# Maxima of four heads in one transfer with early fills, and one division per pair of heads: a decoder layer on one core

## Chip, cores and metric

One core of a Trainium2 chip. The metric is the device time of one execution in microseconds, median over the runs; lower is better. Before the change: 663.38 us, median of three runs (662.83, 663.38 and 667.53).

## What is computed

A decoder layer on x of shape (4, 1024, 256): windowed causal self-attention, cross-attention to 77 context rows, and a fake-quantised feed-forward part, each with a layer norm in front and added to x. Cut to what matters here:

```
# self-attention: 16 heads of 16, windows of 128, keys of this window and the one before
scores = einsum('bhcqd,bhckd->bhcqk', qc, kcat) / 4
scores = where(mask, scores, -inf)
attn   = softmax(scores, axis=-1)
out    = einsum('bhcqk,bhckd->bhcqd', attn, vcat)
x      = x + out @ w_out
# cross-attention: the same with 77 context rows as keys, a mask and biases
# feed-forward: quantised gate, up and down products
```

The softmax is computed as exp(score - max of its row), and the sum of a row comes out of the product with the values, as one more column of ones; the result is divided by it at the end.

## The kernel before

**Jobs, units, slots.** Attention is eight jobs in the order S0, S1, S2, X0, S3, X1, X2, X3: self-attention (S) and cross-attention (X) of the four batch entries. A job has two groups g of eight heads; in a group, head 2j + o lies in partitions 32j + 16o to 32j + 16o + 15, so o = 0 or 1 tells the even from the odd heads, and four heads (j = 0 to 3) run side by side on TensorE, each on 32 rows. A unit is (job, g, o, u): u runs over four quarters of the sequence in an S job and two halves in an X job. That makes 96 units, and slot n works on unit n. Within a slot the order of instructions on all engines is written out: products of weights and values that are due (weighted_values, normalise, by_features), then tasks by due time (project, values, out_project, transposes of x), then statistics and other DVE work beside, then put_maxima, then the maxima of the unit five slots ahead (LEAD = 5), then the weights of this slot's unit. A planner picks tasks by due time and cost; most of them come well ahead of their use.

**Maxima as a row of q.** The subtraction of the maximum is done by the product itself. For the heads of o, one row of each 32 (row 16 for o = 0, row 0 for o = 1) is free: q holds the negated maxima there and k holds ones. So a unit's scores are computed twice: in maxima (sc_n, query rows in partitions, line 735 for S and 750 for X) to find the largest score per query on DVE (lines 765 and 776), and in weights (sc_t, transposed, lines 827 and 856) with the maxima already in the product, followed by the exponential on ScalarE. While the maxima are sought, the free row must add nothing: q or k is zero in it.

**project** (line 346) computes q or k of one group and one half of the sequence. ScalarE copies the product twice: once whole and once with all rows but those of o set to zero (lines 377 and 378; for the q of an X job lines 364 and 367). For X jobs the zeros and ones of the free rows are filled here by two transfers per half (line 371).

**put_maxima** (line 784) runs once per (job, g, o), one slot (S) or three (X) before the first unit that needs it: TensorE turns the maxima into 32 rows of 128 (ps_mx), ScalarE copies them to mxT, and SyncE's queue sends, for S jobs, one fill of ones into k (line 793, four rows of 4 KB), then one transfer for each of the four heads j into its row of q (line 801, 4 KB each). All these transfers go through SyncE, one after another.

**weighted_values, normalise, by_features** (lines 862, 897, 912). The product with the values (ps_av) comes out with features in partitions. DVE transposes it in 32x32 blocks (o_sb, line 895), takes the reciprocal of the sums (rec, line 903), multiplies (aN, line 905), and after o = 1 transposes aN back (aT, line 917), which out_project (line 919) multiplies by the output weights. All of it stands at the head of a slot, ahead of the DVE reductions of that slot's maxima. o_sb has one buffer, aN two. In the last slots (tail) the multiplication goes to GpSimd.

PSUM has eight banks in rotation for all products, so that a product waits for the engine that reads the bank's old content.

Of the kernel before, what the change touches and what calls it, by code (L numbers as in the profile page):

```python
# [9 lines left out]
F32 = mybir.dt.float32  # L10
# [3 lines left out]
AF = mybir.ActivationFunctionType  # L14
ALU = mybir.AluOpType
# [3 lines left out]
P = 128  # L19
# [6 lines left out]
def decoder_layer(  # L26
# [44 lines left out]
    HS = S // NH  # L71
# [130 lines left out]
    with ExitStack() as att:  # L202
# [14 lines left out]
        rows, onerow, nextrow = [], [], []  # L217
# [68 lines left out]
        class Job:  # L286


            def __init__(self, kind, b):
                self.kind, self.b = kind, b  # L290
                self.leads = (kind, b) == ("S", 0)
                self.st = {}
                self.xn, self.xnT, self.vs, self.q, self.k = {}, {}, {}, {}, {}
                self.aN, self.aT, self.mx, self.pts, self.av = {}, {}, {}, {}, {}

            def branch(self):
                twin = copy.copy(self)
# [33 lines left out]
        def normed_T(job, hf):  # L331
# [11 lines left out]
                    nc.scalar.copy(xnT[:, c, :], ps)  # L343
            job.xnT[hf] = xnT

        def project(job, g, which, hf):
# [15 lines left out]
            half = [out[g, o][:, hf * HS : (hf + 1) * HS] for o in range(NS)]  # L362
            if job.kind == "X":
                nc.scalar.activation(
                    half[1], ps, AF.Identity, bias=job.bq[:, g : g + 1], scale=QSCALE
                )
                nc.scalar.activation(
                    half[0], half[1], AF.Identity, bias=nextrow[0], scale=rows[0]
                )
                for row in range(2):  # L370
                    queue_of[0].dma_start(
                        out=half[1][row : P : SL, :].rearrange("j (t q) -> j t q", q=P),
                        in_=none_one[row].unsqueeze(1).to_broadcast([NJ, HT, P]),
                    )
                return
            first = 1 if which == "q" else 0
            nc.scalar.activation(half[first], ps, AF.Copy, scale=QSCALE if which == "q" else 1.0)  # L377
            nc.scalar.activation(half[1 - first], half[first], AF.Copy, scale=rows[1 - first])


        leading = Job("S", 0)
# [34 lines left out]

        begun = dict(turn)
        begin.close()
        queue_of = [nc.sync]

        def attention(alike):
            turn.update(begun)
            queue_of[0] = nc.sync if alike else nc.scalar
# [360 lines left out]
            def put_maxima(job, g, o):  # L784

                ps = bank("ps_mx")
                nc.tensor.transpose(
                    ps[: NJ * NT, :P], job.mx[g, o].rearrange("p j t -> p (j t)"), ident
                )
                mxT = work.tile([NJ * NT, P], F32, name="mxT", tag="mxT", bufs=2)  # L790
                nc.scalar.copy(mxT, ps[: NJ * NT, :P])  # L791
                if job.kind == "S":
                    queue_of[0].dma_start(
                        out=job.k[g, o][(1 - o) * HD : P : SL, :].rearrange(
                            "j (t q) -> j t q", q=P
                        ),
                        in_=none_one[1].unsqueeze(1).to_broadcast([NJ, NT, P]),
                    )
                for j in range(NJ):
                    row = j * SL + (1 - o) * HD  # L800
                    queue_of[0].dma_start(
                        out=job.q[g, o][row : row + 1, :],
                        in_=mxT[j * NT : (j + 1) * NT, :],
                    )

            def weight_bias(job, g, o, u):

# [8 lines left out]
            def weights(job, g, o, u):  # L816
# [34 lines left out]
                else:  # L851
# [5 lines left out]
                    for j in range(NJ):  # L857
                        pt = work.tile([SK, HS], F32, name="ptx", tag="pt", bufs=16)
                        nc.scalar.activation(pt, banks[j][:SK], AF.Exp)  # L859
                        job.pts[g, o, j, u] = pt  # L860

            def weighted_values(job, g, o, hf):
                ps = bank("ps_av")
                heads = [2 * NJ * g + 2 * j + o for j in range(NJ)]
                if job.kind == "S":
                    t0 = hf * HT
                    for kb in range(max(t0 - 1, 0), t0 + HT):

                        a0, a1 = max(kb, t0), min(kb + 2, t0 + HT)
                        for j in range(NJ):  # L870
                            nc.tensor.matmul(  # L871
                                ps[j * SL : (j + 1) * SL, (a0 - t0) * P : (a1 - t0) * P],
                                slot_of(job.vs[kb // 2][:, kb % 2], heads[j]),
                                job.pts[g, o, j, kb // 2][:, kb % 2, a0 - kb : a1 - kb, :],
                                start=(kb == max(t0 - 1, 0)),
                                stop=True,
                                skip_group_check=True,
                            )
                else:
                    for j in range(NJ):  # L880
                        nc.tensor.matmul(  # L881
                            ps[j * SL : (j + 1) * SL, :],
                            slot_of(vx[:, job.b], heads[j]),
                            job.pts[g, o, j, hf],
                            start=True,
                            stop=True,
                        )

                if job is jobs[-1] and (g, o, hf) == (NP - 1, NS - 1, NH - 1):
                    job.av[g, o, hf] = next_of("xnT", xnTs)[  # L890
                        :, 0, :
                    ]
                else:
                    job.av[g, o, hf] = work.tile([P, HS], F32, name="o_sb", tag="o_sb", bufs=1)
                nc.vector.transpose(job.av[g, o, hf], ps)  # L895

            def normalise(job, g, o, hf, tail):

                if o == 0:
                    job.aN[g, hf] = work.tile([P, HS], F32, name="aN", tag="aN", bufs=2)  # L900
                on = job.av[g, o, hf].rearrange("p (s e) -> p s e", e=SL)
                rec = small.tile([P, HS // SL, 1], F32, name="rec")
                nc.vector.reciprocal(rec, on[:, :, HD : HD + 1])
                aN = job.aN[g, hf].rearrange("p (s e) -> p s e", e=SL)
                (nc.gpsimd if tail else nc.vector).tensor_tensor(
                    aN[:, :, o * HD : (o + 1) * HD],
                    on[:, :, 0:HD],
                    rec.to_broadcast([P, HS // SL, HD]),
                    ALU.mult,
                )  # L910

            def by_features(job, g, o, hf):

                if o == NS - 1:
                    if g == 0:
                        job.aT[hf] = work.tile([P, NC, HS], F32, name="aT", tag="aT", bufs=3)
                    nc.vector.transpose(job.aT[hf][:, g, :], job.aN[g, hf])  # L917
# [313 lines left out]
            for slot in range(first, last):  # L1231
# [378 lines left out]
```

## Time and profile before

| | us |
|---|---|
| median of three runs | 663.38 |
| the profiled execution | 661.71 |
| its span, first to last instruction | 660.0 |
| TensorE busy in it | 607.4 |
| VectorE (DVE) busy in it | 541.5 |
| ScalarE (ACT) busy in it | 366.8 |
| GpSimd (POOL) busy in it | 268.6 |

Attention lies between about 18 and 540 us of the span, the feed-forward part behind it. In the profile PE is TensorE's matmul, PEld its loading of weights, SPq SyncE's queue, and L765 is line 765. A row of a timeline has start, length, engine, line, operation, output<-inputs, shapes and count, and in brackets the idle time before it with what ended it. A row of groups has count, then busy us and mean ns of one, then idle us before them and what ended it. The mean granted clock of TensorE over the span is 0.986 of full speed.

### The profile page before, as it was taken

How to read it: one execution, taken by the hardware profiler on the slowest of the kernel's cores; microseconds unless marked ns; L12 is line 12 of the kernel's file. 1: busy time of each engine (PE TensorE's matmuls, PEld its weight loads, DVE VectorE, ACT ScalarE, POOL GpSimd, SP SyncE). 2: the span in 40 equal slices, each digit the busy share in tenths (PEclk: the TensorE clock that was granted, in tenths of full speed). 3: DMA queues.
4: the chain of work that ended last, by engine and by line, in shares of the span. 5: the costliest groups of instructions: out<-in, count | busy, mean ns of one | idle time of the engine just before them, and what ended most of it. 6: DMA issues, size and time to landing. Idle time of an engine off the chain costs nothing.

```text
span 660.0 us, 20192 instructions
## 1 busy us (share of the span) xinstructions
PE 607.4 (92%) x7862; PEld 347.5 (53%) x7862; DVE 541.5 (82%) x1915; ACT 366.8 (56%) x672; POOL 268.6 (41%) x522
## 2 busy tenths in 40 slices
PE   9899999999999989989999999999999997878774
PEld 6456556566565655544456655544434345334564
DVE  5778878788689798578997986888878787799896
ACT  2365655644656536455565365447466565698392
POOL 3164633645227487440064866526601141111032
PEclk9999999999999999799999999999999999899898
DMA  8100100000000000000000000000000110000057
GB/s 289 51 5 16 38 4 20 4 5 23 3 28 12 11 12 14 5 22 18 5 11 11 13 26 28 5 4 6 4 4 6 35 65 17 1 0 1 1 96 164
DMA packets 19293, 17.93 MB, mean 27 GB/s; under 512 B 3190, under 2 KB 18551, under 8 KB 19191
## 3 DMA queue, kind: packets, MB, share of 16 engines
q1 hardware_dynamic: 16999, 14.74, 7.0%
q0 software_dynamic: 1904, 1.84, 2.1%
q8 instruction: 64, 1.05, 0.6%
q14 instruction: 38, 0.31, 0.1%
q10 hardware_dynamic: 288, 0.00, 0.0%
HBM read 9.47 MB, written 6.03 MB: 23 GB/s over the span
## 4 chain that ended last, share of the span: by engine, by line
PE 56%; DVE 30%; ACT 6%; issue 6%; POOL 1%; DMA 1%; DVEq 0%; ACTq 0%
PE ps_p L306 11%; PE ps_av L871 7%; PE sc_n L735 7%; PE sc_t L827 6%; PE ps_op L306 6%; DVE junk L765 5%; PE ps_av L881 3%; DVE o_sb L895 3%; PE ps_v L306 3%; DVE bnst L192 2%; PE sc_n L750 2%; PE sc_t L856 2%; DVE aT L917 2%; PE ps_idle L117 2%; DVE x L935 2%
## 5 line engine op out<-in xcount | busy, mean ns | idle before, releaser
L765 DVE CUSTOM_DVE_ANT_0 junk<-sc_n,cboth 128x256 bf16<-128x256 f32 (+1 forms) x512 | 172.7, 403 | 33.1 <-PE sc_n L735 32.7
L837 ACT ACTIVATE pt<-sc_t 128x512 f32<-128x512 f32 (+1 forms) x256 | 125.4, 577 | 84.3 <-PE sc_t L827 83.1
L841 POOL TENSOR_SCALAR_AFFINE_SELECT pt<-pt 128x256 f32<-128x256 f32 x256 | 101.7, 407 | 113.1 <-ACT pt L837 102.9
L859 ACT ACTIVATE ptx<-sc_t 77x512 f32<-77x512 f32 x128 | 65.2, 596 | 36.1 <-PE sc_t L856 36.1
L827 PE MATMUL sc_t<-shared 32*128 32x256 f32 (+1 forms) x1024 | 79.8, 371 | 2.9 <-DMA shared<-mxT 1.8
L735 PE MATMUL sc_n<-shared 32*128 32x256 f32 (+1 forms) x1024 | 75.1, 387 | 2.7 <-ACT shared L377 1.2
L322 POOL TENSOR_SCALAR xn<-x,mv,rs 128x256 f32<-128x256 f32 x56 | 69.7, 1251 | 0.0
L827 PEld LDWEIGHTS sc_t<-shared 32*128 32x128 f32 x1024 | 61.6, 186 | 11.0 <-ACT mxT L791 2.7
L160 POOL TENSOR_SCALAR ve<-mv 128x4 f32<-128x4 f32 x20 | 4.6, 232 | 153.3 <-DVE mv L194 153.3
L895 DVE STREAM_TRANSPOSE o_sb<-ps_av 128x512 f32<-128x512 f32 x63 | 45.0, 714 | 24.4 <-PE ps_av L871 15.3
L306 PE MATMUL ps_p<-shared,w_s 128*32 128x512 f32 x512 | 60.9, 595 | 3.3 <-DVE mx L776 1.7
L735 PEld LDWEIGHTS sc_n<-shared 32*128 32x128 f32 x1024 | 46.1, 184 | 33.3 <-DVE mx L765 12.6
L871 PE MATMUL ps_av<-pt,vt 128*32 128x256 f32 (+1 forms) x1152 | 60.3, 353 | 3.0 <-DVE mx L765 2.6
L776 DVE TENSOR_REDUCE mx<-sc_n 128x4 f32<-128x308 f32 x128 | 51.8, 467 | 8.7 <-PE sc_n L750 8.5
L871 PEld LDWEIGHTS ps_av<-pt,vt 128*32 128x32 f32 x1152 | 35.5, 112 | 31.9 <-issue 6.9
L765 DVE DVE_READ_ACCUMULATOR2_ANT mx<- 128x1 f32 x512 | 42.9, 84 | 0.0
L856 PE MATMUL sc_t<-shared,kx 32*77 32x512 f32 x256 | 42.8, 598 | 0.0
L377 ACT ACTIVATE shared<-ps_p 128x512 f32<-128x512 f32 x32 | 19.1, 597 | 38.7 <-PE ps_p L306 38.7
L881 PE MATMUL ps_av<-ptx,vx 77*32 77x512 f32 x256 | 36.0, 605 | 4.8 <-DVE mx L776 3.1
L750 PEld LDWEIGHTS sc_n<-kx,shared 32*128 32x128 f32 x1024 | 31.7, 186 | 10.2 <-DVE mv L194 1.7
L750 PE MATMUL sc_n<-kx,shared 32*128 32x77 f32 x1024 | 36.4, 277 | 0.0
L1423 ACT ACTIVATE act<-pg,gsc 128x512 f32<-128x512 f32 x44 | 29.2, 687 | 11.6 <-PE pg L1408 8.9
(200 smaller groups left out, 990.7 us busy)
## 6 DMA issues: line engine op xcount, KB each, us to landing
x<-in_x_dram SPq DMA_DIRECT2D x8, 512.0 KB
out_dram<-shared SPq DMA_DIRECT2D x9, 256.0 KB
shared<-mxT SPq DMA_DIRECT2D x128, 4.0 KB
out_dram<-x SPq DMA_DIRECT2D x7, 256.0 KB
out_dram<-shared POOLq DMA_DIRECT2D x7, 256.0 KB, 4.5
w_s<-in_L_attn_w_qkv_dram SPq DMA_DIRECT2D x2, 384.0 KB
raw_d<-in_L_ffn_w_down_dram SPq DMA_DIRECT2D x2, 352.0 KB
raw_f<-in_L_ffn_w_gate_dram SPq DMA_DIRECT2D x5, 128.0 KB
```

The source lines that it names most:

```text
L306: nc.tensor.matmul(out[r], lhsT[:, r], rhs, skip_group_check=True, **on)
L322: eng.tensor_scalar(xn, xb[job.b][:, t, :], job.st[hf].mv[:, i, 0:1], job.st[hf].rs[:, i : i + 1], ALU.subtract, ALU.mult,)
L735: nc.tensor.matmul(banks[j][:, (i + 1) * 2 * P - n : (i + 1) * 2 * P], q[r, t * P : (t + 1) * P], k[r, k0 * P : k0 * P + n], start=True, s ...
L750: nc.tensor.matmul(banks[j][:, i * SK : (i + 1) * SK], q[r, t * P : (t + 1) * P], k[r, :], start=alike, stop=alike or i == HT - 1,)
L765: nc.vector.tensor_tensor_reduce(out=junk[:, 2 * P - n :], in0=banks[j][:, (i + 1) * 2 * P - n : (i + 1) * 2 * P], in1=cboth[:, 2 * P - n ...
L827: nc.tensor.matmul(banks[j][:, w : w + n], k[r, t * P : (t + 1) * P], q[r, t * P : t * P + n], start=True, stop=True,)
L837: nc.scalar.activation(pt.rearrange("p i a q -> p (i a q)")[:, :w], banks[j][:, :w], AF.Exp)
L841: nc.gpsimd.affine_select(out=pt[:, :, 0, :], in_=pt[:, :, 0, :], compare_op=ALU.is_ge, fill=0.0, base=0, pattern=[[0, 2], [1, P]], channe ...
L856: nc.tensor.matmul(banks[j][:SK], k[r, :], q[r, s], start=alike, stop=True)
L859: nc.scalar.activation(pt, banks[j][:SK], AF.Exp)
L871: nc.tensor.matmul(ps[j * SL : (j + 1) * SL, (a0 - t0) * P : (a1 - t0) * P], slot_of(job.vs[kb // 2][:, kb % 2], heads[j]), job.pts[g, o, ...
L895: nc.vector.transpose(job.av[g, o, hf], ps)
```

## The change

1. The four transfers of maxima become one, from the 32 rows of mxT into the four rows of q.
2. The fill of ones into k leaves put_maxima. Instead project sets the free rows of S jobs at once: for k, the odd heads' copy gets its ones by a bias in ScalarE's second copy, and the even heads' by a transfer of half a row each (fill); for q, row 0 of the odd heads' copy is filled with zeros, since k holds ones there from now on while the maxima are sought. The first projections are filled through SyncE's queue too, before attention begins.
3. Where the mask's rows are alike (as here), and for all jobs but the last, o_sb becomes a tile for both o, with two buffers. After o = 1 one reciprocal and one multiplication serve the pair (normalise_pair), and they and the transpose by_features stand at the end of the slot, behind the reductions of its maxima and behind its weights. aN has one buffer for them. The last job divides each o as before, with o_sb and aN as the two halves of one tile.

```diff
+        def fill(half, row, value):
+            queue_of[0].dma_start(
+                out=half[row : P : SL, :].rearrange("j (t q) -> j t q", q=P),
+                in_=none_one[value].unsqueeze(1).to_broadcast([NJ, HT, P]),
+            )
...
             first = 1 if which == "q" else 0
             nc.scalar.activation(half[first], ps, AF.Copy, scale=QSCALE if which == "q" else 1.0)
-            nc.scalar.activation(half[1 - first], half[first], AF.Copy, scale=rows[1 - first])
+            if which == "q":
+                nc.scalar.activation(half[0], half[1], AF.Copy, scale=rows[0])
+                fill(half[1], 0, 0)
+            else:
+                nc.scalar.activation(
+                    half[1], half[0], AF.Identity, bias=onerow[1], scale=rows[1]
+                )
+                fill(half[0], HD, 1)
...
                 nc.scalar.copy(mxT, ps[: NJ * NT, :P])
-                if job.kind == "S":
-                    queue_of[0].dma_start(
-                        out=job.k[g, o][(1 - o) * HD : P : SL, :].rearrange(
-                            "j (t q) -> j t q", q=P
-                        ),
-                        in_=none_one[1].unsqueeze(1).to_broadcast([NJ, NT, P]),
-                    )
-                for j in range(NJ):
-                    row = j * SL + (1 - o) * HD
-                    queue_of[0].dma_start(
-                        out=job.q[g, o][row : row + 1, :],
-                        in_=mxT[j * NT : (j + 1) * NT, :],
-                    )
+                queue_of[0].dma_start(
+                    out=job.q[g, o][(1 - o) * HD : P : SL, :].rearrange(
+                        "j (t q) -> j t q", q=P
+                    ),
+                    in_=mxT,
+                )
...
+            def apart(job):
+                return job is jobs[-1] or not alike
...
-                else:
+                elif not alike:
                     job.av[g, o, hf] = work.tile([P, HS], F32, name="o_sb", tag="o_sb", bufs=1)
+                else:
+                    if o == 0:
+                        job.pair[g, hf] = work.tile(
+                            [P, NS, HS], F32, name="o_sb", tag="o_sb", bufs=2
+                        )
+                    job.av[g, o, hf] = job.pair[g, hf][:, 0 if apart(job) else o, :]
                 nc.vector.transpose(job.av[g, o, hf], ps)
...
+            def normalise_pair(job, g, hf):
+
+                aN = job.aN[g, hf] = work.tile([P, HS], F32, name="aN", tag="aN", bufs=1)
+                on = job.pair[g, hf].rearrange("p o (s e) -> p o s e", e=SL)
+                rec = small.tile([P, NS, HS // SL, 1], F32, name="rec2", bufs=1)
+                nc.vector.reciprocal(rec, on[:, :, :, HD : HD + 1])
+                nc.vector.tensor_tensor(
+                    aN.rearrange("p (s o d) -> p o s d", o=NS, d=HD),
+                    on[:, :, :, 0:HD],
+                    rec.to_broadcast([P, NS, HS // SL, HD]),
+                    ALU.mult,
+                )
...
                     for args in values_of.get(slot, ()):
                         weighted_values(*args)
+                        if not apart(args[0]):
+                            continue
                         normalise(*args, tail)
...
                     weights(*now)
+                for job, g, o, hf in values_of.get(slot, ()):
+                    if o == NS - 1 and not apart(job):
+                        normalise_pair(job, g, hf)
+                        by_features(job, g, o, hf)
                 for fn, args in late.get(slot, ()):
```

More of the change, by code (lines that the diff above doesn't have):

```diff
@@ L294, in __init__ @@
                 self.aN, self.aT, self.mx, self.pts, self.av = {}, {}, {}, {}, {}
+                self.pair = {}
             def branch(self):
@@ L344, in normed_T @@
             job.xnT[hf] = xnT
+        queue_of = [nc.sync]
+        def fill(half, row, value):
[3 more added lines that the diff above has]
+            )
         def project(job, g, which, hf):
@@ L369, in project @@
                 )
-                for row in range(2):
-                    queue_of[0].dma_start(
-                        out=half[1][row : P : SL, :].rearrange("j (t q) -> j t q", q=P),
-                        in_=none_one[row].unsqueeze(1).to_broadcast([NJ, HT, P]),
-                    )
+                fill(half[1], 0, 0)
+                fill(half[1], 1, 1)
                 return
@@ L377, in project @@
             nc.scalar.activation(half[first], ps, AF.Copy, scale=QSCALE if which == "q" else 1.0)
-            nc.scalar.activation(half[1 - first], half[first], AF.Copy, scale=rows[1 - first])
+            if which == "q":
+                nc.scalar.activation(half[0], half[1], AF.Copy, scale=rows[0])
+                fill(half[1], 0, 0)
+            else:
[3 more added lines that the diff above has]
+                fill(half[0], HD, 1)
         leading = Job("S", 0)
@@ L418, in decoder_layer @@
         begin.close()
-        queue_of = [nc.sync]
         def attention(alike):
@@ L791, in put_maxima @@
                 nc.scalar.copy(mxT, ps[: NJ * NT, :P])
-                if job.kind == "S":
-                    queue_of[0].dma_start(
-                        out=job.k[g, o][(1 - o) * HD : P : SL, :].rearrange(
-                            "j (t q) -> j t q", q=P
-                        ),
-                        in_=none_one[1].unsqueeze(1).to_broadcast([NJ, NT, P]),
-                    )
-                for j in range(NJ):
-                    row = j * SL + (1 - o) * HD
-                    queue_of[0].dma_start(
-                        out=job.q[g, o][row : row + 1, :],
-                        in_=mxT[j * NT : (j + 1) * NT, :],
-                    )
+                queue_of[0].dma_start(
[4 more added lines that the diff above has]
+                )
             def weight_bias(job, g, o, u):
@@ L892, in weighted_values @@
                     ]
-                else:
-                    job.av[g, o, hf] = work.tile([P, HS], F32, name="o_sb", tag="o_sb", bufs=1)
+                elif not alike:
+                    job.av[g, o, hf] = work.tile([P, HS], F32, name="o_sb", tag="o_sb", bufs=1)
+                else:
+                    if o == 0:
[3 more added lines that the diff above has]
+                    job.av[g, o, hf] = job.pair[g, hf][:, 0 if apart(job) else o, :]
                 nc.vector.transpose(job.av[g, o, hf], ps)
@@ L899, in normalise @@
                 if o == 0:
-                    job.aN[g, hf] = work.tile([P, HS], F32, name="aN", tag="aN", bufs=2)
+                    if alike:
+                        job.aN[g, hf] = job.pair[g, hf][:, 1, :]
+                    else:
+                        job.aN[g, hf] = work.tile([P, HS], F32, name="aN", tag="aN", bufs=2)
                 on = job.av[g, o, hf].rearrange("p (s e) -> p s e", e=SL)
```

## The prediction, made before the changed kernel ran

> **What bounds the kernel now.** I read the page's busy shares and its chain first, then busy time by stretch, then the timeline where the tensor engine stands still, and last the groups by shape.
>
> ```profile
> PE 607.4 (92%) x7862; PEld 347.5 (53%) x7862; DVE 541.5 (82%) x1915; ACT 366.8 (56%) x672; POOL 268.6 (41%) x522
> ...
> PE 56%; DVE 30%; ACT 6%; issue 6%; POOL 1%; DMA 1%; DVEq 0%; ACTq 0%
> ```
>
> TensorE carries the chain, with DVE between its pieces. The change lives in attention; the next view is busy time by stretch (length, then PE, PEld, DVE, ACT, POOL busy, granted clock).
>
> ```profile
> 18.00:540.00 522.00, 500.79 (x7121) 279.22 (x7122) 429.05 (x1713) 285.94 (x564) 241.89 (x476) 0.99 0.05 15
> 263.14:266.55 3.41, 2.09 (x38) 1.59 (x39) 1.63 (x4) 1.50 (x2) 0.82 (x2) 1.00 0.04 12
> 266.55:273.38 6.83, 6.83 (x56) 4.24 (x57) 1.08 (x3) 2.06 (x4) 2.32 (x5) 0.50 0.02 5
> ```
>
> In 522 us of attention PE idles 21 us, and that is nearly all that can be won there. The second and third lines show one transfer wait (PE busy 2.09 of 3.41 us) and behind it 6.83 us at half clock. The timeline names the wait:
>
> ```profile
> 261.87 0.56 SPq L793 DMA_DIRECT2D shared<-fill  x1
> 262.52 2.75 SPq L801 DMA_DIRECT2D shared<-mxT  x4
> ...
> 265.46 3.14 PE L827 MATMUL sc_t<-shared 32*128 32x256 f32 x16 [1.30 <-DMA shared<-mxT]
> ```
>
> SyncE spends 0.56 us on the fill and 2.75 us on four rows of maxima, one after another; sc_t, 1.04 us elsewhere, starts 1.30 us late and takes 3.14. From the trace's completion signals: the 128 single rows landed 1.79 us (median) after their issue began, the 16 whole fills (4 rows x 4 KB) 2.33, the 32 half fills of the X jobs 1.91.
>
> **Part 1: one transfer for the maxima.** It has the destination shape of the whole fill, so I price it at 2.33 us (ends: 1.79, the single row; 4.5, what fill and four rows take now). SyncE issues 96 fewer of them, and off PE's path that is worth nothing.
> - At 264: the S job's fill is gone from here, so the transfer goes out at 261.87 and lands at 264.20; sc_n ends at 264.15. Gain 1.30 + (3.14 - 1.04) - 0.05 = 3.3 us, and without the wait no half clock: 4.9 us of work behind sc_t ran at half speed, 2.4 us more.
> - At 396 the same pattern: 0.48 idle, and sc_t takes 3.04 for 1.04; issued at 393.25 it lands by 395.6. Gain 2.4.
> - Four first sc_t groups of a head group are stretched (35.5: 1.81, 181.2: 1.45, 221.0: 1.30, 353.0: 1.37): together 1.8.
> Sum -9.9 us; if it landed no sooner than now, 0.
>
> The row for the transfer's shape stands above. The Trainium skill ("DMA: Bandwidth & Descriptors", on how many engines a transfer uses, and its rules for kernel authors) says that an outermost dimension of c under 16 confines a transfer to at most c engines, so four here, which speaks against merging. By the faster row, 1.79, the sum would be better by about 0.1 us only.
>
> **Part 2: early fills.** The ones of k and the zeros of q move from behind the maxima to the projection: 32 half fills in place of 16 whole ones, ahead of the loads in SyncE's order, and the second k copy takes a bias (+0.09 us on ACT, 813 for 722 ns). Now sc_n waits for the fill, and the fill for both copies. Six of the eight S projections of k have a slot (some 5 us) or more between copy and first use, against 1.91 + 0.05: nothing. Two have not, both in the slot that uses them:
>
> ```profile
> 24.77 2.01 PE L735 MATMUL sc_n<-shared 32*128 32x256 f32 x32 [0.74 <-ACT shared L377]
> ...
> 314.63 0.60 ACT L377 ACTIVATE shared<-ps_p 128x512 f32<-128x512 f32 x1 [0.78 <-PE ps_p L306]
> 315.26 0.72 ACT L378 ACTIVATE shared<-shared,rows 128x512 f32<-128x512 f32 x1
> 315.28 1.15 PE L735 MATMUL sc_n<-shared 32*128 32x256 f32 x16 [0.50 <-ACT shared L377]
> ```
>
> sc_n starts as soon as the first k copy is done. At 315 it must wait for the second (ends 316.07), the issue and 1.91 us: 318.03, so +2.75. At the start there are two in a row: half 0's fill (k copied by 18.12, landing 20.1, sc_n was at 18.64) costs 1.5, or 2.2 if it queues behind the last packet of x (20.34); half 1's copies end at 27.05, landing at 29.0 for 24.77: in all +4.25. Behind sc_n, PE's queue holds sc_t and the next products, and DVE waits for the scores, so nothing covers it. Ends: 5 to 8.5 for both; I take 7.0.
>
> **Part 3: one division per pair.**
>
> ```profile
> L905 DVE TENSOR_TENSOR aN<-o_sb,rec 128x256 f32<-128x256 f32 x57 | 25.1, 440 | 2.0
> L903 DVE RECIPROCAL rec<-o_sb 128x16 f32<-128x16 f32 x63 | 16.0, 254 | 2.1
> L1538 DVE TENSOR_TENSOR shared<-shared,x 128x512 f32<-128x512 f32 x9 | 6.2, 692 | 0.3
> L611 DVE RECIPROCAL winv<-gsc 128x1 f32<-128x1 f32 x6 | 1.0, 165 | 0.2
> ```
>
> A reciprocal costs 165 ns at one element and 254 at 16, 5.9 ns each, so 349 at 32 (ends 254 and 508). The product of 512 takes 692. A pair goes from 2 x (254 + 440) = 1388 to 1041 ns; over 28 pairs (7 jobs x 2 x 2) DVE loses 9.7 us. The last job keeps its single ones. What PE sees is the order: division and transpose now stand ahead of the maxima of their slot, past which (and past the copies, sums and statistics beside them) they move. Where PE waits, e.g.
>
> ```profile
> 285.21 1.92 PE L306 MATMUL ps_p<-shared,w_s 128*32 128x512 f32 x16 [1.67 <-DVE mx L776]
> ```
>
> DVE had 1.6 us of division in its unbroken run before that mx. I went through PE's gaps over 0.1 us between 18 and 540 us: they sum to 20.5, and those that follow a division in the same DVE run to 8.7, with 1.6 more inside a stretched sc_n at 62. I take -8 of these 10.3, since part of the wait turns up behind the moved block; ends -3 (the shortening alone, a third of it on the path) and -14.7 (with the 4.4 us of gaps in slots that have no division).
>
> The move adds a wait: aT is ready only 349 + 692 + 711 = 1.75 us after the slot's last maximum, and out_project reads it. In the schedule that the planner writes, all but three first out_projects come two or more slots later; these three come in the very next one.
>
> ```profile
> 411.43 0.25 DVE L903 RECIPROCAL rec<-o_sb 128x16 f32<-128x16 f32 x1
> 411.72 0.57 DVE L905 TENSOR_TENSOR aN<-o_sb,rec 128x256 f32<-128x256 f32 x1
> 412.32 0.71 DVE L917 STREAM_TRANSPOSE aT<-aN 128x512 f32<-128x512 f32 x1
> ...
> 414.63 1.62 DVE L776 TENSOR_REDUCE mx<-sc_n 128x4 f32<-128x308 f32 x4
> 415.15 1.93 PE L306 MATMUL ps_op<-wo_s,aT 128*32 128x256 f32 x32
> ```
>
> Here mx could start at 413.8 (sc_n done) and end at 415.4; aT at 417.15; ps_op waits 2.1 us, with sc_n and sc_t queued behind it. At 507.75 likewise 2.2. At 464.84 DVE runs unbroken from 455 and has two divisions less ahead, so 0. Sum +4.3 (ends 0 and 6.5).
>
> **Part 4: the clock.** Four new waits of PE over 2 us: 3.5 (at 25), 3.3 (at 315), 2.1 and 2.2. The row above shows 1.3 us idle plus a stretched group followed by 6.83 us at half speed; a gap of 1.67 at 283.5 did not. A halving costs at most 6.83 / 2 = 3.4. I take 1.2 at the start (PE has 1.17 us to spare there before DVE's last maximum), 2.0 at 315, 0.8 for the others: +4, ends 0 and 13.6. The Trainium skill ("TensorE: Matmul & The Clock Gate", Part 1) says the clock halves after at least one idle window of about 3.4 us. By that rule the first two waits could hardly fill a window and part 4 would be 0, the sum -6.6 and the forecast 657; the trace's window was 61% busy, so I go by the row.
>
> **Sum**: -9.9 + 7.0 - 8 + 4.3 + 4 = -2.6 on the profiled execution's 661.7 (span 660.0 and 1.7 around): 659.1. The median of the runs shown is 1.7 above that execution: 661.
>
> **Rivals.**
> - Slower, by the clock: every one of the four waits halves it for the full 6.83 us. Part 4 is then 13.6: 661 + 9.6 = 671. For it: a window 61% busy sufficed. Against: gaps of 1.67 at 283.5 and of 2.05 at 579.3 and 593.2 cost no clock. It needs three of the four to pass 670.
> - Faster: DVE's waits go nearly whole (-12) and only one wait halves the clock (part 4 is 1, not 4), and the reciprocal stays at 254 ns (28 x 0.095 = 2.7): 661 - 4 - 3 - 2.7 = 651. For it: DVE's 429 of 522 us with runs of 10 us unbroken. Against: 1.75 us of DVE lands in front of the next transpose of ps_av, whose bank PE wants back.
> - The change does not do what it says: four rows on few engines land as late as now. Part 1 falls to 0: 671. Against: the whole fill's 2.33 us in 16 cases out of 16 (at most 2.71).
>
> **Chances.** Forecast 0.51 (own range 655 to 668), clock rival 0.21, faster rival 0.23, the last 0.05. Within 1% (6.6 us) a measurement of this kernel can't tell much from no change. Under 656.7: the faster rival and 0.04 of the forecast, 0.27. Over 670.0: most of the clock rival and of the last, and a little of the forecast's tail, 0.22. That leaves 0.51. Range 649 to 673: the faster rival at 651, those two at 671, and the unknowns' ends partly cancelling.
>
> **What will show it.** sc_t at the two changes from an S to an X job 1.04 us long, no half clock near 266; 32 issues for the maxima. sc_n waiting for a fill once at the start (some 29 us) and once near 315. DVE's reciprocal of 128x32 near 349 ns and product near 692. ps_op waiting for aT twice. The prediction is wrong if other sc_n groups wait for fills, if ps_op waits in more than three places, or if half clock appears in more than three stretches of attention.

## The result and the profile after

| | before | after |
|---|---|---|
| median, us | 663.35 (6 runs, 662.38 to 667.53) | 681.69 (6 runs, 678.49 to 686.21) |
| ratio, 95% interval | | 1.0281 [1.0251, 1.0311] |
| the profiled execution, us | 661.71 | 683.0 |
| its span, us | 660.0 | 681.1 |
| mean granted clock | 0.986 | 0.975 |
| half clock in attention, us | 6.8 | 23.9 |

The change made the kernel slower by 2.8%, 18.3 us. The prediction of 661 us and its range up to 673 were wrong. The first view is the page of the changed kernel: busy time, the chain, and the four groups whose idle time moved most.

```profile
PE 610.7 (90%) x7857; PEld 346.4 (51%) x7862; DVE 534.0 (78%) x1859; ACT 368.8 (54%) x672; POOL 272.2 (40%) x522
...
PE 56%; DVE 28%; ACT 6%; issue 6%; DMA 2%; POOL 1%; SPq 0%; DVEq 0%; ACTq 0%
...
L776 DVE CUSTOM_DVE_ANT_0 junk<-sc_n,cboth 128x256 bf16<-128x256 f32 (+1 forms) x512 | 172.7, 403 | 56.1 <-PE sc_n L746 55.6
...
L746 PE MATMUL sc_n<-shared 32*128 32x256 f32 (+1 forms) x1024 | 77.6, 398 | 9.5 <-DMA shared<-fill 9.2
L831 PE MATMUL sc_t<-shared 32*128 32x256 f32 (+1 forms) x1024 | 77.2, 369 | 5.3 <-DVE shared L342 2.8
...
L878 PE MATMUL ps_av<-pt,vt 128*32 128x256 f32 (+1 forms) x1152 | 58.6, 346 | 9.3 <-DVE mx L776 8.8
```

DVE lost 7.5 us of work and gained idle time: in front of the maxima of the S jobs (junk, line 765 before, 776 now) it waits 56.1 us, nearly all of it for sc_n, where the same group of before waited 33.1. DVE is not short of time as a whole; it waits for PE more and PE waits for it more: sc_t for DVE's copy of xnT (line 342), ps_av for the last maximum (8.8 us, 2.6 before). And sc_n waits for fills (9.2). The two groups of before to compare with:

```profile
L765 DVE CUSTOM_DVE_ANT_0 junk<-sc_n,cboth 128x256 bf16<-128x256 f32 (+1 forms) x512 | 172.7, 403 | 33.1 <-PE sc_n L735 32.7
...
L871 PE MATMUL ps_av<-pt,vt 128*32 128x256 f32 (+1 forms) x1152 | 60.3, 353 | 3.0 <-DVE mx L765 2.6
```

The second view is the busy time by stretch of the changed kernel (columns as before): attention, two windows ahead of a half clock, and two at half clock.

```profile
18.00:552.00 534.00, 497.57 (x7082) 275.58 (x7086) 414.71 (x1636) 281.34 (x550) 241.55 (x465) 0.98 0.05 15
...
424.60:428.00 3.40, 2.31 (x40) 1.26 (x32) 3.30 (x9) 2.47 (x6) 2.60 (x4) 1.00 0.04 10
428.00:431.40 3.40, 2.79 (x28) 1.04 (x28) 0.56 (x1) 0.00 (x0) 3.40 (x6) 0.50 0.02 5
520.20:523.60 3.40, 1.60 (x18) 0.42 (x16) 3.26 (x10) 2.48 (x6) 0.00 (x0) 0.99 0.00 0
...
523.60:533.80 10.20, 9.01 (x81) 3.92 (x85) 6.89 (x16) 2.30 (x5) 0.00 (x0) 0.50 0.01 3
```

PE is now idle 36.4 us of the 534 (21.2 of 522 before). The half clock of before at 266 is gone; there are new ones at 28.6 (3.4 us), 322.2 (6.8), 428.0 (3.4) and 523.6 (10.2).

The third view is the timeline of PE in the changed kernel at five places that the prediction named.

```profile
28.30 3.53 PE L746 MATMUL sc_n<-shared 32*128 32x256 f32 x32 [3.56 <-DMA shared<-fill]
...
271.56 1.50 PE L831 MATMUL sc_t<-shared 32*128 32x256 f32 x16
...
322.84 2.09 PE L746 MATMUL sc_n<-shared 32*128 32x256 f32 x16 [3.36 <-DMA shared<-fill]
...
428.61 2.79 PE L307 MATMUL ps_op<-wo_s,aT 128*32 128x256 f32 x24 [1.64 <-DVE aT L946]
...
524.79 2.79 PE L307 MATMUL ps_op<-wo_x,aT 128*32 128x256 f32 x24 [1.39 <-DVE aT L946]
```

The wait for the maxima's transfer (264 before, 271.56 here) is gone, and the waits for fills and for aT stand where they were forecast. So the large miss lies in places that no step of the prediction named. To find them I compared when each of the 7862 weight loads of PE starts in the two traces; their order is the same but for one swapped pair. I call this comparison the alignment of a trace with before. The difference stands at +3.5 us at 36, grows in small jumps to +11.8 by 258, falls to +4.4 by 285 at the first change from an S to an X job, and stands at +19.8 at 530. The jumps, 1.0 to 1.7 us each, sit in the S slots without values that follow a slot with a pair; over all of attention they add to about 14, with small gains of 0.6 to 0.9 between them. At three of these places sc_t waits 0.91 to 0.93 us for the copy of line 342; at four others ps_av waits 1.1 to 1.3 us for the last maximum. The next two views show one such place on DVE and PE, before and after.

```profile
77.04 0.25 DVE L903 RECIPROCAL rec<-o_sb 128x16 f32<-128x16 f32 x1
...
77.33 0.42 DVE L905 TENSOR_TENSOR aN<-o_sb,rec 128x256 f32<-128x256 f32 x1
...
77.79 0.71 DVE L917 STREAM_TRANSPOSE aT<-aN 128x512 f32<-128x512 f32 x1
...
79.73 0.42 DVE L765 CUSTOM_DVE_ANT_0 junk<-sc_n,cboth 128x256 bf16<-128x256 f32 x1 [0.59 <-PE sc_n L735]
...
82.49 0.69 DVE L341 COPY shared<-ps_t 128x512 f32<-128x512 f32 x1
...
83.40 1.23 PE L827 MATMUL sc_t<-shared 32*128 32x256 f32 x15
...
83.49 0.42 DVE L765 CUSTOM_DVE_ANT_0 junk<-sc_n,cboth 128x256 bf16<-128x256 f32 x1 [0.31 <-PE sc_n L735]
```

Before, division and transpose (77.04 to 78.50) run while PE does a projection and sc_n, and DVE still waits 0.59 us for the scores: they lie in a hole. In the slot behind, the copy at 82.49 is early enough; sc_t waits for nothing, and DVE for sc_n. The same two slots after the change:

```profile
82.26 0.42 DVE L776 CUSTOM_DVE_ANT_0 junk<-sc_n,cboth 128x256 bf16<-128x256 f32 x1 [2.08 <-PE sc_n L746]
...
85.02 0.35 DVE L933 RECIPROCAL rec<-o_sb 128x32 f32<-128x32 f32 x1
...
85.41 0.86 DVE L934 TENSOR_TENSOR aN<-o_sb,rec 128x512 f32<-128x512 f32 x1
...
86.30 0.71 DVE L946 STREAM_TRANSPOSE aT<-aN 128x512 f32<-128x512 f32 x1
86.94 0.65 DVE L342 COPY shared<-ps_t 128x512 f32<-128x512 f32 x1
...
87.64 1.13 PE L831 MATMUL sc_t<-shared 32*128 32x256 f32 x12 [0.93 <-DVE shared L342]
```

The hole is only deeper (2.08 for 0.59), since PE is no earlier. The block now stands from 85.02 to 86.94 between the maxima of one slot and the copy of the next, where DVE had 0.31 us to spare. sc_t waits 0.93 for the copy, the eight maxima start late, and PE is put back 1.7 us.

That is theory P: what costs is the place behind the maxima, ahead of a slot that has no room. Its rivals are F (the early fills, with the clock) and Q (the pairing itself, its longer pieces on DVE).

### The profile page after: what moved, and what is told of

It is laid out like the page before. It is cut to its first block, busy times and chain, and to the rows that moved or that the text cites. A ratio compares the mean times of both kernels' runs of the same rounds, so it can differ in the third digit from the quotient of the medians.

```text
span 681.1 us, 19935 instructions
## 1 busy us (share of the span) xinstructions
PE 610.7 (90%) x7857; PEld 346.4 (51%) x7862; DVE 534.0 (78%) x1859; ACT 368.8 (54%) x672; POOL 272.2 (40%) x522
## 4 chain that ended last, share of the span: by engine, by line
PE 56%; DVE 28%; ACT 6%; issue 6%; DMA 2%; POOL 1%; SPq 0%; DVEq 0%; ACTq 0%
PE ps_p L307 10%; PE ps_av L878 8%; PE ps_op L307 7%; PE sc_n L746 6%; DVE junk L776 6%; PE sc_t L831 4%; PE ps_av L888 3%; PE ps_v L307 3%; PE sc_n L761 3%; PE sc_t L860 3%; DVE bnst L192 2%; DVE aT L946 2%; DVE aN L934 2%; DVE mx L787 2%; PE pg L1443 2%
## 5 line engine op out<-in xcount | busy, mean ns | idle before, releaser
L776 DVE CUSTOM_DVE_ANT_0 junk<-sc_n,cboth 128x256 bf16<-128x256 f32 (+1 forms) x512 | 172.7, 403 | 56.1 <-PE sc_n L746 55.6
L746 PE MATMUL sc_n<-shared 32*128 32x256 f32 (+1 forms) x1024 | 77.6, 398 | 9.5 <-DMA shared<-fill 9.2
L831 PE MATMUL sc_t<-shared 32*128 32x256 f32 (+1 forms) x1024 | 77.2, 369 | 5.3 <-DVE shared L342 2.8
L323 POOL TENSOR_SCALAR xn<-x,mv,rs 128x256 f32<-128x256 f32 x56 | 72.6, 1302 | 0.0
L746 PEld LDWEIGHTS sc_n<-shared 32*128 32x128 f32 x1024 | 48.2, 190 | 39.9 <-issue 17.1
L878 PE MATMUL ps_av<-pt,vt 128*32 128x256 f32 (+1 forms) x1152 | 58.6, 346 | 9.3 <-DVE mx L776 8.8
L831 PEld LDWEIGHTS sc_t<-shared 32*128 32x128 f32 x1024 | 59.5, 185 | 13.3 <-DVE shared L342 4.0
L888 PE MATMUL ps_av<-ptx,vx 77*32 77x512 f32 x256 | 37.7, 633 | 3.6 <-DVE mx L787 3.4
L964 DVE TENSOR_TENSOR x<-x,ps_op 128x512 f32<-128x512 f32 x28 | 19.1, 683 | 24.7 <-PE ps_op L307 24.7
L761 PEld LDWEIGHTS sc_n<-kx,shared 32*128 32x128 f32 x1024 | 32.5, 190 | 10.7 <-issue 1.7
```

The costliest lines, as they stand in the source:

```text
L323: eng.tensor_scalar(xn, xb[job.b][:, t, :], job.st[hf].mv[:, i, 0:1], job.st[hf].rs[:, i : i + 1], ALU.subtract, ALU.mult,)
L746: nc.tensor.matmul(banks[j][:, (i + 1) * 2 * P - n : (i + 1) * 2 * P], q[r, t * P : (t + 1) * P], k[r, k0 * P : k0 * P + n], start=True, s ...
L761: nc.tensor.matmul(banks[j][:, i * SK : (i + 1) * SK], q[r, t * P : (t + 1) * P], k[r, :], start=alike, stop=alike or i == HT - 1,)
L776: nc.vector.tensor_tensor_reduce(out=junk[:, 2 * P - n :], in0=banks[j][:, (i + 1) * 2 * P - n : (i + 1) * 2 * P], in1=cboth[:, 2 * P - n ...
L831: nc.tensor.matmul(banks[j][:, w : w + n], k[r, t * P : (t + 1) * P], q[r, t * P : t * P + n], start=True, stop=True,)
L878: nc.tensor.matmul(ps[j * SL : (j + 1) * SL, (a0 - t0) * P : (a1 - t0) * P], slot_of(job.vs[kb // 2][:, kb % 2], heads[j]), job.pts[g, o, ...
```

## Experiments

All ratios are against the kernel before, run beside. "Half clock" is that in attention, in the profiled execution alone, which need not be the median one.

**1. The division half alone.** The changed kernel with `put_maxima` and the fills of before:

```diff
-                queue_of[0].dma_start(
-                    out=job.q[g, o][(1 - o) * HD : P : SL, :].rearrange(
-                        "j (t q) -> j t q", q=P
-                    ),
-                    in_=mxT,
-                )
+                if job.kind == "S":
...
+                for j in range(NJ):
+                    row = j * SL + (1 - o) * HD
+                    queue_of[0].dma_start(
+                        out=job.q[g, o][row : row + 1, :],
+                        in_=mxT[j * NT : (j + 1) * NT, :],
+                    )
```

> The pair division behind the slot's maxima, with the transfers and fills of before. Theory P (position: the block of reciprocal, product and transpose, 1.9 us, now stands on DVE ahead of the copies, sums and maxima of the next slot, which has no products with values and where DVE had no time to spare): 672 to 681 us against 663, with PE waiting 0.9 to 1.3 us on DVE in about ten slots that follow a pair and about 1.5 us on aT in three. Rival F (the early fills and the half clock they bring cost the time; the division is harmless): 656 to 665 us, and no such waits.

682.34 us (679.33 to 682.96), ratio 1.0273 [1.0239, 1.0308], half clock 23.9 us: 1.3 us above P's range and far from F's. This half alone carries as much as the whole; F can't be the cause.

**2. The transfer half alone.** The kernel before with the one transfer and the early fills, divisions untouched.

> One transfer for the maxima and early fills, with the division of before. Theory P: the gains (sc_t at the two changes from S to X jobs, some 9 us with the clock) and the costs (start 3.5, the same-slot fill near 315 some 3 us and a half clock behind it, two weight loads that are late by 1 us each) nearly cancel: 660 to 667 us. Rival F: 678 to 684 us.

666.68 us (664.27 to 670.21), 1.0053 [1.0032, 1.0074], half clock 17.1 us: within P's range.

**3. The pair divided in place.** As run 1, with the block at the head of the odd heads' slot, where the single division stood:

```diff
                         if not apart(args[0]):
+                            job, g, o, hf = args
+                            if o == NS - 1:
+                                normalise_pair(job, g, hf)
+                                by_features(job, g, o, hf)
                             continue
...
-                for job, g, o, hf in values_of.get(slot, ()):
-                    if o == NS - 1 and not apart(job):
-                        normalise_pair(job, g, hf)
-                        by_features(job, g, o, hf)
```

> One division per pair, but at the head of the slot of the odd heads where the single ones stood; transfers and fills of before. Theory P: DVE loses 28 x 0.24 = 6.7 us of work and nothing is moved behind the maxima: 658 to 663 us, no waits on aT. Rival Q (the pair itself costs: the wider product at 0.80 us and a heavier block for the odd heads): 666 to 675 us.

669.76 us (666.66 to 670.77), 1.0083 [1.0054, 1.0112]: a miss for P, whose 658 to 663 was too low, and within Q's range. But 12.6 of run 1's 18.9 us go with the place alone. Its windows show where much of the remaining 6.3 comes from:

```profile
282.60:286.00 3.40, 1.39 (x24) 0.56 (x20) 3.33 (x9) 1.64 (x4) 3.40 (x7) 1.00 0.10 27
286.00:292.80 6.80, 6.80 (x70) 3.05 (x64) 2.33 (x8) 2.77 (x6) 2.27 (x2) 0.50 0.06 22
```

The wait for mx that was 1.67 us at 283.5 before is 2.01 here, and now 6.8 us at half clock follow; another 6.8 follow the transfer wait at 400. Half clock is 17.1 us in all for 6.8, some 5 us of time.

**4. One transfer, late fill.** Only the four transfers become one; the fill stays in front of it.

> The four transfers of maxima merged into one and nothing else; the fill of ones stays in front of it. Theory P: sc_t at the two changes from S to X jobs waits some 0.7 us where it waited 3.4 and 2.5, one issue of 0.54 us and a landing 2.3 us after it: 656 to 660 us, no half clock near 266. Rival F (merging itself is worth nothing, its gain came from the fill leaving): 662 to 664 us.

656.79 us (654.74 to 658.45), 0.9909 [0.9886, 0.9933], no half clock; within P's range. So Part 1 is worth 6.6 us, and the early fills cost 9.9 of run 2.

**5. The place without the pairing.** The kernel before; its single divisions, and by_features, stand at the end of their slots.

```diff
                         weighted_values(*args)
+                        if args[0] is not jobs[-1]:
+                            continue
                         normalise(*args, tail)
...
                     weights(*now)
+                for args in values_of.get(slot, ()):
+                    if args[0] is not jobs[-1]:
+                        normalise(*args, tail)
+                        by_features(*args)
```

> The kernel before with its two single divisions per pair kept, but each of them, with the transpose by_features behind o = 1, moved to the end of its slot behind the maxima and the weights (the last job as before); transfers of before. Theory P (the place behind the maxima is what costs: 682.3 with the pair moved, 669.8 with the pair in place, so some 12.6 us): 673 to 682. Rival Q (the pairing costs, by its longer unbroken piece on VectorE): 661 to 666.

672.16 us (670.32 to 678.14; before 662.26), 1.0176 [1.0135, 1.0216]: 9.9 us, just under P's range and far from Q's. In its profiled execution (670.32, the fastest of the four and 8.6 us over that of before) half clock is 6.8 us as before, so this much is lost with the clock's share unchanged; 2.9 us of it are the three waits for aT (1.07, 1.30 and 0.57). Its timeline at the same two slots:

```profile
82.34 0.71 DVE L917 STREAM_TRANSPOSE aT<-aN 128x512 f32<-128x512 f32 x1
...
82.98 0.65 DVE L341 COPY shared<-ps_t 128x512 f32<-128x512 f32 x1
...
83.69 1.13 PE L827 MATMUL sc_t<-shared 32*128 32x256 f32 x12 [0.39 <-DVE shared L341]
```

The single block is 1.38 us where the pair's is 1.92, and sc_t waits 0.39 where it waits 0.93: the wait follows the block's length to the hundredth. At the two other places where sc_t waits for the copy behind a pair (0.92 and 0.91 us), it waits 0.39 behind the single block too. At the place shown PE is put back 1.2 us, for 1.7 with the pair: each time the block less the 0.31 that DVE had to spare, and 0.1.

**6. All pairs behind but three.** As run 1, but the three pairs whose aT the very next slot multiplies are divided in place (`at_once`).

```diff
+            def at_once(job, g, hf):
+                return g == 1 and hf == 0 and (job.kind, job.b) in (("S", 3), ("X", 1), ("X", 2))
```

> The division half alone (682.3), but the three pairs whose aT is multiplied in the very next slot (the second groups of S3, X1 and X2, first half) divided in place ahead of the maxima. If the waits for aT and the half clock behind them cost what the alignment of the two traces showed (1.8 + 1.1 near 415, 1.6 near 465, 2.2 + 2.8 near 508, in all 9.5, part of it the clock), 673 to 676, with two stretches of half clock fewer. If the loss lies in the other slots and these waits only take the place of others: 679 to 682.

675.66 us (674.27 to 679.5), 1.0192 [1.0166, 1.0217]: 13.4 us over before, where run 1 is 18.9 over its own. The waits for aT and what follows them are worth about 5.5, known to some 3 us either way. Half clock is still 20.5 us, now at other places, so the forecast of two stretches fewer was a miss.

**7. One slot later.** As run 6, but the block stands at the end of the slot behind its own (`values_of.get(slot - 1, ())`), so that in the S jobs it comes ahead of a slot with values.

> As moved_but_three, but every other pair's division stands one slot later, behind the maxima of the slot after it, so that in the S jobs it falls ahead of a slot that has values again. Theory P in its narrow form (the slots without values have no room on VectorE, those with values have): below moved_but_three by 6 to 10 us, 664 to 669. In its wide form (any slot whose copies and maxima are put back loses the same): within 2 us of moved_but_three.

664.50 us (661.28 to 665.33), 1.0027 [1.0011, 1.0044]: 11.2 us less than run 6 with the same instructions, of which up to 5.1 is half clock (10.2 us for 20.5). The narrow form of P holds. The timeline, same two slots and the head of the next:

```profile
80.28 0.69 DVE L342 COPY shared<-ps_t 128x512 f32<-128x512 f32 x1
...
81.19 1.23 PE L831 MATMUL sc_t<-shared 32*128 32x256 f32 x15
81.28 0.42 DVE L769 CUSTOM_DVE_ANT_0 junk<-sc_n,cboth 128x256 bf16<-128x256 f32 x1 [0.31 <-PE sc_n L739]
...
84.04 0.35 DVE L936 RECIPROCAL rec<-o_sb 128x32 f32<-128x32 f32 x1
...
86.89 0.29 DVE L769 CUSTOM_DVE_ANT_0 junk<-sc_n,cboth 128x128 bf16<-128x128 f32 x1 [0.26 <-PE sc_n L739]
```

The copy is early again, sc_t waits for nothing. The same block lies from 84.04 to 86.03, and behind it DVE still waits 0.26 for the next sc_n: here there is room for it.

**8. Pair in place with one transfer** (runs 3 and 4 together).

> The pair's division in place (669.8 with the transfers of before) with the four maxima transfers made one and the fill left in front (656.8 alone). If the pair's 6.3 us in place are mostly half clock behind transfer waits near 283 and 396 (17 us of half clock for 6.8), then without those waits it is 656 to 659, and no half clock in attention. If pairing costs by VectorE's order itself, the two add: 662 to 664.

659.64 us (657.6 to 662.29), 0.9956 [0.9938, 0.9974]; half clock 6.8 us. Just over the lower range and below the upper: pairing in place costs about 3 us more than run 4, half of what it cost in run 3. The wait near 283 that the expectation counts among the transfer waits is one for mx (run 3's windows), which one transfer doesn't take away, and a stretch of half clock, 3.4 us, follows there again (280.6). What the other half is stays open.

**9. One slot later with one transfer** (runs 7 and 4 together).

> The pair's division one slot later (664.5 with the transfers of before) with the four maxima transfers made one and the fill left in front (656.8 alone). If what the pair still costs there (2.2) is mostly half clock behind the transfer wait near 396 (6.8 us of it), 655 to 658, level with or below 656.8; if the two simply add, 659.

657.31 us (656.36 to 658.85), 0.9913 [0.9890, 0.9936], half clock 3.4 us: level with run 4. Its alignment with before stands at -10.7 us by 285 and at -6.0 by 519, so nearly half of what the S jobs gain the later jobs give back; why they do is not shown.

**10. Early fills only where there is room.** As run 2, but the first groups of S0 and S3 keep the late fill.

```diff
+        def late_fill(job, g):
+            return job.kind == "S" and g == 0 and job.b in (0, 3)
```

> The transfer half alone (666.7), but the first groups of S0 and S3, whose k is multiplied in the slot that projects it, keep the late fill of before; the other six S groups keep the early ones. If early fills cost only at those two places and the clock behind them, as the prediction said (6 of 8 cost nothing), 656 to 659, level with the late fills' 656.8, with at most the 1.2 to 1.5 us of the weight load that stands behind a fill near 123. If they cost throughout by their place ahead of the loads in SyncE's queue, 661 to 666.

654.69 us (653.67 to 657.38), 0.9873 [0.9848, 0.9898], half clock 3.4 us; 1.3 us below the lower range. 12 us of run 2 go with two of its eight groups. The other six fills cost nothing net. Three rows of its timeline:

```profile
124.15 0.63 PE L496 MATMUL ps_w<-ident,raw_w 128*128 128x128 f32 x4 [1.57 <-DMA raw_w<-in_L_xattn_Wv_dram]
...
263.18 0.53 SPq L815 DMA_DIRECT2D shared<-mxT  x1
...
265.35 1.11 PE L843 MATMUL sc_t<-shared 32*128 32x256 f32 x16
```

The transfer issued at 263.18 no longer makes sc_t wait. The first row is a cost that stayed: the load of raw_w is now queued behind a fill on SyncE's queue, and PE waits 1.57 us for it.

**11. The pair later in the first three jobs.** Transfers of run 10, pairs one slot later in S0, S1 and S2, single divisions in the five other jobs.

```diff
             def apart(job):
-                return job is jobs[-1] or not alike
+                return not alike or job not in jobs[:3]
```

> The transfers as in early_where_room (654.7); the pair's division one slot later, as in one_slot_later, in S0, S1 and S2 alone, and two single divisions as before in the five other jobs. The alignment of one_slot_later_one_transfer with before stands at -10.7 us by 285 and gives back 5 of it in the jobs behind; that of early_where_room stands at -4.4 by 273. If the pair one slot later relieves the S jobs and only the later jobs give it back, 649 to 652. If the relief is lost again whatever stands behind, 654 to 657.

650.76 us (650.3 to 652.17; before 662.89), 0.9823 [0.9794, 0.9851], no half clock in attention. It is faster than the kernel before by 1.8% and than the change by 4.5% (650.76 to 681.69), with the same two ideas. The alignment stands at -9.6 us by 285, near run 9's -10.7, and this time stays there: -10.9 at 530. Whether two single divisions one slot later would gain as much was not run, so what of this is the pairing stays open.

## Why the prediction was wrong, point by point

**The step that failed** is in Part 3: "I take -8 of these 10.3, since part of the wait turns up behind the moved block; ends -3 ... and -14.7". It counted the waits behind the old place as gain, and let at most a part come back. The runs show the opposite sign: the move costs 9.9 us with single divisions (run 5) and, with the three waits for aT taken out, 13.4 with pairs (run 6, part of it half clock). Of run 5's 9.9 some 2.9 are waits for aT, so the place itself costs some 6 to 7 us where 8 were to be won. Some of the counted waits did go: the 1.67 us before 285.21, the prediction's own example, is gone in the changed kernel and in run 1, and in run 1's alignment the gains come to about 5 us; the new place costs more than that. Nor did the shortening alone gain the 3 us of the near end: the pair in place costs 6.3 us (run 3), and some 3 with one transfer (run 8). Two readings were wrong in it. A wait that follows a division in an unbroken DVE run was taken to shrink by the division; but a stretch earlier on DVE had a hole in which the division lay free (0.59 us of waiting behind it at 79.73), and taking it out made the hole 2.08. And the new place was priced at nothing: "1.75 us of DVE lands in front of the next transpose of ps_av" stood only as an argument against the faster rival. It is not that transpose but the next slot's copy, in a slot without values, where the trace of before shows 0.31 us to spare for a block of 1.92. That row was there to be read; both ends of the term lay below zero without a reason that excluded a loss.

**Division's durations.** The reciprocal took 347 ns for 349. The product took 800 for 692, and the groups by shape show what of it is the place, first in the changed kernel, then with the pair in place:

```profile
L934 DVE TENSOR_TENSOR aN<-o_sb,rec 128x512 f32<-128x512 f32 x28 | 22.4, 800 | 1.0
...
L933 DVE RECIPROCAL rec<-o_sb 128x32 f32<-128x32 f32 x28 | 9.7, 347 | 0.0
```

```profile
L934 DVE TENSOR_TENSOR aN<-o_sb,rec 128x512 f32<-128x512 f32 x28 | 19.5, 698 | 1.0
```

So DVE saved 6.7 us in divisions, not 9.7; in run 7 the product took 803 and the time was good, so this term did not decide.

**Waits for aT.** Forecast 2.1, 0 and 2.2, sum 4.3; the trace has 1.64, 1.20 (at 480) and 1.39, sum 4.2. Right as a sum, but the 0 was wrong. With the clock behind them they are worth 5.5 (run 6).

**Part 1**, -9.9: the mechanism was right in the main: the wait at 264 and the half clock behind it went. At 396 a wait for the transfer stays (0.43 us in the changed kernel, 0.48 before), but sc_t takes 1.15 us for 3.04. The 32 transfers landed 1.86 us (median) after their issue began, between the ends of 1.79 and 4.5 and better than the 2.33 taken. Worth: 6.6 [4.4, 7.6], so it was over-priced by some 3 us. In run 4's profiled execution, aligned with before, the place at 264 gained 4.5 for 5.7, that at 396 1.6 for 2.4, and all before 262, the stretched groups among it, 1.3. The Trainium skill's rule ("DMA: Bandwidth & Descriptors", its rules for kernel authors) that an outermost dimension of four keeps a transfer to at most four engines cost nothing that can be seen here: 16 KB in 1.86 us against 4 KB in 1.79.

**Part 2**, +7.0 and 3.2 of clock: right in sum; how it divides between waits and clock was not measured. Early fills cost 9.9 (run 2 over run 4), and without the two places named nothing is left of it (run 10). Not seen: the load of raw_w behind a fill; the prediction set "ahead of the loads in SyncE's order" down without pricing it. It costs 1.2 to 1.6 us near 124.

**Part 4**, +4: too low. There were four stretches of half clock, 23.9 us in all; the PE work in these stretches ran at half speed, so at most 10.7 us (half of the 21.4 that PE was busy in them). The clock rival (13.6, total 671) was nearer, but alone it does not reach 682. "A halving costs at most 6.83 / 2 = 3.4" was wrong too: at 523.6 the stretch lasted 10.2. That stretch, moreover, does not follow the forecast wait alone. The wait for aT begins at 523.40, and the window ahead is idle mostly by a wait for the last maximum that no step named; the first row is the changed kernel's, the second that of before:

```profile
521.90 1.07 PE L888 MATMUL ps_av<-ptx,vx 77*32 77x512 f32 x8 [1.61 <-DVE mx L787]
```

```profile
506.51 1.07 PE L881 MATMUL ps_av<-ptx,vx 77*32 77x512 f32 x8 [0.91 <-ACT ptx L859]
```

**The sum.** Against -2.6, the whole is +18.3. The transfer half was forecast at about 0 and measured +3.3; the division half was forecast at about -3 and measured +18.9. Together they would be 22.2; whole they are 3.9 less, in line with the merged transfer taking away the half clock that run 1 shows at 275, which no run isolates.

## What to carry to other kernels

Before moving a block within an engine's order, read the idle row in front of what followed it at the old place (if the engine waited there anyway, the block was free) and the idle row behind the new place (its length less that idle is about what PE was put back at the place shown, with the pair's block and with the single one). A mean share of busy time says neither: DVE fell from 82% to 78% busy and the kernel lost 18 us. The same block one slot further on cost 2.2 us in place of 13.4, so try neighbouring places before giving up an idea, and only in the stages that have room.

## What the chip showed that was not expected

**The half clock starts on a grid.** In every trace here the starts of half clock lie whole multiples of 3.413 us apart within the run (in the changed kernel 0, 86, 117, 145 times), and a stretch lasted 3.4, 6.8 or 10.2 us. PE's busy time in the window ahead does not decide alone: in the profile of run 3, the window ahead of the stretch at 402 was nearly full,

```profile
398.60:402.00 3.40, 3.01 (x42) 1.86 (x38) 1.63 (x4) 1.50 (x2) 3.40 (x5) 1.00 0.22 76
402.00:408.80 6.80, 6.80 (x60) 3.58 (x62) 0.77 (x2) 2.07 (x4) 2.51 (x6) 0.50 0.02 5
```

3.01 us busy of 3.40 (the last 1.7 of it by six products of sc_t, of which sixteen take 1.04 us elsewhere), while windows of before and of run 4 with 1.83 and 1.74 us busy were not followed by half clock. What decides was not found. The Trainium skill ("TensorE: Matmul & The Clock Gate", Part 1) names an idle window of about 3.4 us in a free-running count: the length and the grid agree, the idleness does not.

**GpSimd delays the product.** Of the 28 products of the pair in the changed kernel, the 9 that met no GpSimd operation took 691 to 695 ns; the 19 others 691 to 1120, mean 851. The longest with its neighbours, from the timeline:

```profile
383.90 0.72 POOL L702 TENSOR_TENSOR x<-x,bo_b 128x256 f32<-128x256 f32 x1
384.05 1.12 DVE L934 TENSOR_TENSOR aN<-o_sb,rec 128x512 f32<-128x512 f32 x1
384.61 1.66 POOL L323 TENSOR_SCALAR xn<-x,mv,rs 128x256 f32<-128x256 f32 x1
```

GpSimd's product ends at 384.62, 0.57 us after DVE's began, and DVE's took 0.43 more than alone; GpSimd's next one, begun under it, took 1.66. Behind the weights the block meets GpSimd's masking of pt (line 845), in place it mostly doesn't (mean 698). The Trainium skill ("SBUF — State Buffer", on its two separate sides) says that a VectorE operation with two SBUF inputs and a GpSimd operation that reads SBUF lock one port pair against each other; these rows agree with a wait for the end of GpSimd's operation to within 0.15 us. It does not hold for every operation of GpSimd: a product that began at 478.48, with 0.87 us of a tensor_scalar still to run, took 745 ns.
